# A state-space layer on one core: a logarithm in place of a polynomial step, a sixth product a chunk on GpSimd, and a new timetable

## The chip, the core and the metric

The kernel runs on one core of one Trainium2 chip. The metric is device time in microseconds of one execution. The kernel before takes 4875.83 us (median of 3 runs, 4874.54 to 4876.55). The engines are named as in the profile: PE (TensorE), DVE (VectorE), ACT (ScalarE), POOL (GpSimd) and SP (SyncE, which here only issues transfers).

## What is computed

Two layers follow each other on x of shape (2, 512, 64, 64). Each is `x = x + layer(groupnorm(x))`. Layer 0 is a selective scan over the 4096 positions of an image, with 1024 channels and 16 states for each channel:

```python
xs = silu(conv1d(layernorm(x) @ in_proj_x))       # z = layernorm(x) @ in_proj_z
dt, B, C = split(xs @ x_proj)
delta = softplus(dt @ dt_proj + dt_bias)
h = exp(delta * A) * h + (delta * xs) * B          # for each position, in order
y = sum_n(h * C) + xs * D
x = x + (y * silu(z)) @ out_proj
```

Layer 1 matches each position with 1024 memory rows (scores, softmax, arg-max), adds the positions into the rows chosen, and multiplies the softmax with the renewed rows. The change leaves layer 1's own code as it was.

## The kernel before

**Tiling of layer 0.** The positions are cut into 32 chunks of 256 (16 for each image; `chunks`, T = 256). Channels lie on the 128 partitions in 8 blocks (`DB`), states in 4 groups of 4 (`G`, `NG`). A *unit* is one channel block and one state group of one chunk: 4 states x 256 positions, a tile of 128x1024. So a chunk has 32 units, and its units are called 0 to 31 here. Blocks go in pairs `p` (8 units each).

**One unit k** takes, in the order of the main loop:

- ACT, `decay(k+1)`: four exponentials write dA of the next unit into PSUM (pool `psa`, two buffers). One unit ahead.
- at the first unit of a pair, `turn`: ACT copies the finished sums yT of the pair before to `ys`, PE transposes them into `py`.
- at unit 2 of a pair (`AT["gate"]`), `gate`: DVE multiplies `py` with silu(z).
- everything that `table` has due at this unit (below).
- DVE, `scan(k)`: `tensor_tensor_scan` runs h = dA*h + bu in place over dA. Then DVE multiplies with C (`weigh`) into `hc` (pool `t2`, two buffers). ACT copies the last column of h to `carry`.
- PE, `gather(k)`: eight transposes of `hc` accumulate in yT.
- POOL, `feed(k+4)`: bu = B * (delta*u) for the unit four ahead (pool `fed`, four buffers, so it must wait for `scan(k)`).
- ACT, `first(k+3)`: copies four first columns into bu.
- POOL, `start`, at units 3, 11, 19, 27: delta*u of the next pair, and its first columns.

**Units set aside.** In units 2, 8, 12, 16 and 26 (`AT["aside"]`) DVE only scans. The scan writes h to an SBUF tile (tag `dS`, one buffer), and POOL multiplies it with C one unit later into an `hc` buffer; PE gathers it right after that unit's own gather.

**Everything else of a chunk** (projections of the next chunk, the norm of the one after it, the output projection of the one before) is cut into parts with due times in units, in the dictionary `AT`; a negative time lies before the chunk's start. `table` is sorted by due time and then priority, and a wrapper (`InOrder`) keeps each engine's instructions in the order in which the loop issues them, SP's transfers too. Parts that matter here: `"u"`, `"z"` (projections on PE, 16 matmuls each), `"c"` (convolutions, 16 matmuls), `"xi"`, `"o"`, `"zo"` (their ACT copies), `"silu"` 9 (ACT loads another function table, takes the silu of z and u, and loads the first table again), `"norm"` (load of x, group norm on ACT in two halves, mean, centre, two squares, variance, root, Newton step, scale), `"back"` (output projection), `"soft"` (delta; its eight times are repeated every 8 units). B and C of the next chunk are loaded at units 26 to 32, as soon as the last reader of each buffer is done.

**delta.** softplus(x) = relu(x) + log(1 + e), e = exp(-|x|). The kernel takes the logarithm on ACT into PSUM (`lg`), and for small e, where 1 + e loses digits, a cubic series; DVE takes the lesser of both (`d_min`). The series is an ACT Square and two POOL instructions (`d_series`). `pd`, `lg` and `py` share one PSUM buffer (pool `psy`, tag `py`).

Of the kernel before, what the change touches and what calls it, by code (L numbers as in the profile page):

```python
# [2 lines left out]

# [6 lines left out]
F32 = mybir.dt.float32  # L10
# [3 lines left out]
AF = mybir.ActivationFunctionType  # L14
ALU = mybir.AluOpType
# [4 lines left out]
P = 128  # L20
# [30 lines left out]
def kernel(  # L51
# [17 lines left out]
    nc = tc.nc  # L69
    B, C, L = x.shape  # L70
    CB = C // P
# [6 lines left out]
    T = 256  # L78
    NCH = L // T
    NG = 4  # L80
# [7 lines left out]
    const = ctx.enter_context(tc.tile_pool(name="const", bufs=1))  # L88
# [16 lines left out]
        out=g3, in_=g3, compare_op=ALU.is_ge, fill=0.0, base=GS - 1,  # L105
        pattern=[[GS, P // GS], [0, GS]], channel_multiplier=-1,
    )
    one = const.tile([P, 1], F32, name="one")
    nc.gpsimd.memset(one, 1.0)
    epsc = const.tile([P, 1], F32, name="epsc")  # L110
    nc.gpsimd.memset(epsc, EPS)
    serb = const.tile([P, 1], F32, name="serb")
    nc.gpsimd.memset(serb, -0.75 * 3.0**-0.5)


    win = const.tile([P, CB, 2 * DI], F32, name="win")
# [8 lines left out]
    xf0 = flat[:, : CB * TT].rearrange("p (c t) -> p c t", t=TT)  # L125
# [4 lines left out]
    gmu = [[const.tile([P, CB], F32, name=f"gmu{i}_{b}") for b in range(B)] for i in range(2)]  # L130
    grs = [[const.tile([P, CB], F32, name=f"grs{i}_{b}") for b in range(B)] for i in range(2)]
# [55 lines left out]
    with ExitStack() as l0:  # L187
        nc = InOrder(tc, tc.nc)
# [1 line left out]


        AT = {
            "u": (-10, -7, -2, 0), "xi": (-9, -6, 1, 2), "c": (-6, -3, 3, 5), "o": (-4, -1, 4, 7),
            "x": 10, "xo": 12, "z": (16, 18, 19, 23), "zo": (18, 19, 22, 27),
            "soft": (20, 21, 22, 22, 22, 24, 25, 26), "silu": 9, "early": -114,
            "aside": (2, 8, 12, 16, 26), "gate": 2,
            "norm": (-1, 0, 3, 8, 10, 10, 11, 14, 15, 17, 18, 18),
            "back": ((0, 6, 8, 10), (1, 13, 14, 15)), "end": 23, "u1": (4, 5, 9, 10),
# [5 lines left out]
        }  # L204
        wp = l0.enter_context(tc.tile_pool(name="w0", bufs=1))
# [4 lines left out]
        t2 = l0.enter_context(tc.tile_pool(name="t2", bufs=2))  # L210
        fed = l0.enter_context(tc.tile_pool(name="fed", bufs=LEAD))
        dl = l0.enter_context(tc.tile_pool(name="dl", bufs=DB // 2 - 1))
        s1 = l0.enter_context(tc.tile_pool(name="s1", bufs=1))
# [36 lines left out]
        U = DB * G  # L250
# [207 lines left out]
        def front(i):  # L458
# [94 lines left out]

            def d_exp(p):
                e = s["e", p]
                nc.scalar.activation(e, e, AF.Exp, scale=-1.0)
                s["q", p] = s1.tile([P, 2, T], F32, tag="q", name="q")
                nc.scalar.activation(s["q", p], e, AF.Square, bias=serb, scale=3.0**-0.5)

            def d_series(p):  # L560
                q = s["q", p]
                engine = nc.vector if i == 0 and p == 0 else nc.gpsimd
                engine.tensor_scalar(q, q, 1.0, 0.8125, ALU.mult, ALU.add)
                engine.tensor_mul(q, q, s["e", p])

            def d_log(p):
                lg = psy.tile([P, 2, T], F32, tag="py", name="lg")
                s["lg", p] = lg
                nc.scalar.activation(lg, s.pop(("e", p)), AF.Ln, bias=one)

            def d_min(p):
                q = s["q", p]
                nc.vector.scalar_tensor_tensor(
                    q, s.pop(("lg", p)), 1.25 * 2.0**-23, q, ALU.add, ALU.min
                )

            def d_sum(p):
# [199 lines left out]
        def prelude():  # L777

            def load_n():
                nc.sync.dma_start(xf0, x1d[0][:, :, :TT])  # L780
                nc.sync.dma_start(mn, mnd)
                nc.sync.dma_start(mrow, m.rearrange("(kb p) c -> p kb c", p=P))

            def norm():
                for cb in range(CB):
                    nc.gpsimd.tensor_scalar(
                        xf0[:, cb], xf0[:, cb], gmu[1][0][:, cb : cb + 1],
                        grs[1][0][:, cb : cb + 1], ALU.subtract, ALU.mult,
                    )

            def turn(i):
                pt = ps.tile([P, 2, T], F32, tag="mm", name="pt")
                pt = pt.rearrange("p a t -> p (a t)")
                for cb in range(CB):
                    nc.tensor.transpose(
                        pt[:, cb * P : (cb + 1) * P], xf0[:, cb, i * P : (i + 1) * P], ident
                    )
                nc.scalar.copy(xT0[:, i], pt)
                junk = s1.tile([P, 2, T], F32, tag="sq", name="junk")
                nc.scalar.activation(  # L800
                    junk.rearrange("p a t -> p (a t)"), xT0[:, i], AF.Square,
                    accum_out=ss0[:, i : i + 1],
                )
# [49 lines left out]
        def early(k):  # L853

            return k % U == AT["early"]

        def aside(k):

            return early(k) or k % U in AT["aside"]

        def decay(k):
            i, db, g = units[k]
# [12 lines left out]
        def scan(k):  # L875
            i, db, g = units[k]
            b, c = chunks[i]
            dA, bu = dAs[k], bus.pop(k)
            if aside(k) and not early(k):
                dAs[k] = s1.tile([P, NG, T], F32, tag="dS", name="h")  # L880
            h = dAs[k]
            nc.vector.tensor_tensor_scan(
                h.rearrange("p n t -> p (n t)"), dA.rearrange("p n t -> p (n t)"),
                bu.rearrange("p n t -> p (n t)"), 0.0, ALU.mult, ALU.add,
            )
            if not aside(k):
                weigh(k, nc.vector)
            if c < NCH - 1:
                nc.scalar.copy(carry[:, db, g * NG : (g + 1) * NG], h[:, :, T - 1])


            if db % 2 == 0 and g == 0:
                pys[i, db // 2] = psy.tile([P, HT, 2, P], F32, tag="yT", name="yT")
            if g == 0:
                for hf in range(HT):
                    nc.tensor.matmul(
                        pys[i, db // 2][:, hf, db % 2], u_of(i, db)[:, hf * P : (hf + 1) * P],
                        dD[:, db], start=db % 2 == 0 and hf == 0, stop=False,
                        skip_group_check=True,
                    )  # L900

        def weigh(k, engine):

            i, db, g = units[k]
            hcs[k] = t2.tile([P, NG, T], F32, tag="hc", name="hc")
            engine.tensor_mul(hcs[k], dAs.pop(k), state[i]["C"][g])

        def gather(k):

            i, db, g = units[k]  # L910
            hc = hcs.pop(k)
            for n in range(NG):
# [120 lines left out]
        for k, (i, db, g) in enumerate(units):  # L1033
            w = k % U
            if k + 1 < n_units and not early(k + 1):
                decay(k + 1)
            if w % (2 * G) == 0 and k > 0:
                turn(*((i, w // (2 * G) - 1) if w else (i - 1, PR - 1)))
            late = i == 0 and w // (2 * G) == 1
            if w % (2 * G) == AT["gate1" if late else "gate"] and k >= 2 * G:  # L1040
                gate(*((i, w // (2 * G) - 1) if w >= 2 * G else (i - 1, PR - 1)))
            while table and table[0][0] <= k:
                table.pop(0)[2]()
            if k + 4 < n_units and early(k + 4):
                decay(k + 4)
            scan(k)
            if k > 0 and aside(k - 1):
                weigh(k - 1, nc.gpsimd)
            for n in (k, k - 1):
                if n in hcs:  # L1050
                    gather(n)
            if k + LEAD < n_units:
                feed(k + LEAD)
            if k + LEAD - 1 < n_units:
                first(k + LEAD - 1)
            if (k + 5) % (2 * G) == 0 and k + 5 < n_units:
                start(units[k + 5][0], units[k + 5][1] // 2)
# [493 lines left out]
```

## Time and profile before

| | |
|---|---|
| median of the runs | 4875.83 us |
| the profiled execution | 4875.14 us |
| its span, first to last instruction | 4872.8 us (2.3 us lie around it) |
| granted clock | 0.981 |
| busy over the span | PE 90%, DVE 87%, POOL 81%, ACT 75% |
| before the first scan | 100.0 us |
| chunk 0 / chunks 1 to 30 / chunk 31 | 143.8 / 3519.4 / 129.2 us |
| after the last scan (mostly layer 1) | 980.4 us |

Names in the profile read `out<-in`: `hc<-dA,C` is the product with C on DVE, `hc<-h,C` the one of a unit set aside on POOL, `dA<-dA,bu` a scan, `h<-dA,bu` the scan of a unit set aside, `bu<-B,du` a feed, `z<-py,z` a gate, `x<-x,pm` the centring of x. L37 is the line of the wrapper, through which nearly everything of layer 0 is issued, so groups are told apart by their tiles. "Idle before" is time in which an engine did nothing ahead of an instruction, put down to what ended it.

### The profile page before, as it was taken

What the parts mean: (1) busy time and instruction counts of PE and PEld (TensorE: products, weight loads), DVE (VectorE), ACT (ScalarE), POOL (GpSimd) and SP (SyncE); (2) the same over time, 40 slices, a digit from 0 to 9 for tenths busy, and PEclk for the clock granted to TensorE, in tenths of its full rate; (3) what the DMA queues carried; (4) which work ended last, traced back from release to release, by engine and by line L of the source; (5) the groups of instructions that cost most, each with busy time, mean ns of one, the idle gap of its engine ahead of it and who ended that gap; (6) DMA issues with size and microseconds to landing.
All of it is one profiled execution on the core that took longest, in us unless ns stands there. A gap on an engine that the chain in (4) does not pass through costs nothing. (4 is left out here: it accounts for less than half of the span.)

```text
span 4872.8 us, 65401 instructions
## 1 busy us (share of the span) xinstructions
PE 4407.3 (90%) x22660; PEld 3440.9 (71%) x22660; DVE 4223.4 (87%) x3538; ACT 3633.0 (75%) x9311; POOL 3971.2 (81%) x2753
## 2 busy tenths in 40 slices
PE   7899999999989999989999899999897799998999
PEld 6777777777777777777777777777776644553444
DVE  6799999999999999999999999999999788887333
ACT  3788888888888888888888888888888555552000
POOL 4799999999999999999999999999999745553121
PEclk9999999999999999999999999999998799999999
DMA  6132222222222222211221122222222134444442
GB/s 220 42 112 70 66 66 66 67 71 70 74 72 70 70 70 72 68 66 66 66 66 66 66 68 73 75 76 73 77 69 87 53 129 164 155 156 162 168 177 104
DMA packets 175348, 439.37 MB, mean 90 GB/s; under 512 B 23688, under 2 KB 78088, under 8 KB 171304
## 3 DMA queue, kind: packets, MB, share of 16 engines
q1 hardware_dynamic: 160456, 366.89, 22.6%
q0 software_dynamic: 10240, 34.61, 2.0%
q10 hardware_dynamic: 4320, 33.69, 1.9%
q8 instruction: 178, 2.92, 0.2%
q14 instruction: 154, 1.26, 0.1%
HBM read 347.44 MB, written 87.69 MB: 89 GB/s over the span
## 5 line engine op out<-in xcount | busy, mean ns | idle before, releaser
L37 POOL TENSOR_TENSOR bu<-B,du 128x1020 f32<-128x1020 f32 (+1 forms) x1151 | 2460.7, 2154 | 131.0 <-DVE dA L37 73.7
L37 ACT ACTIVATE dA<-delta,A 128x256 f32<-128x256 f32 x4096 | 1957.0, 478 | 137.9 <-DVE hc L37 32.9
L37 DVE TENSOR_TENSOR_SCAN dA<-dA,bu 128x1024 f32<-128x1024 f32 x864 | 1975.7, 2287 | 24.8 <-ACT dA L37 18.2
L37 PE MATMUL yT<-ident,hc 128*128 128x128 f32 x8192 | 1076.4, 278 | 185.1 <-DVE hc L37 110.8
L37 DVE TENSOR_TENSOR hc<-dA,C 128x1024 f32<-128x1024 f32 x864 | 1058.3, 1225 | 112.9 <-PE yT L37 18.6
L37 PEld LDWEIGHTS yT<-ident,hc 128*128 128x128 f32 x8192 | 941.8, 143 | 299.7 <-DVE hc L37 153.7
L37 PE MATMUL pz<-x,win 128*128 128x256 f32 x4096 | 942.3, 384 | 21.6 <-ACT carry L37 19.6
L37 PEld LDWEIGHTS pz<-x,win 128*128 128x128 f32 x4096 | 769.1, 193 | 125.3 <-ACT carry L37 25.9
L37 PE MATMUL cv<-xi,cd 128*128 128x256 f32 x2048 | 468.6, 381 | 32.1 <-ACT xi L37 30.3
L37 PE MATMUL po<-z,wo 128*128 128x256 f32 x2048 | 472.9, 384 | 0.8 <-DVE z L37 0.8
L37 PEld LDWEIGHTS cv<-xi,cd 128*128 128x128 f32 x2048 | 379.5, 190 | 88.2 <-ACT xi L37 37.2
L37 PEld LDWEIGHTS po<-z,wo 128*128 128x128 f32 x2048 | 386.6, 193 | 53.7 <-DVE z L37 1.0
L37 POOL TENSOR_TENSOR hc<-h,C 128x1024 f32<-128x1024 f32 x160 | 385.0, 2407 | 3.9 <-PE yT L37 3.9
L37 DVE TENSOR_TENSOR_SCAN h<-dA,bu 128x1024 f32<-128x1024 f32 x160 | 364.4, 2278 | 3.6 <-ACT dA L37 3.6
L37 ACT COPY carry<-dA 128x4 f32<-128x4 f32 x810 | 128.6, 159 | 226.4 <-DVE hc L37 220.1
L37 PE MATMUL py<-ident,ys 128*128 128x128 f32 x512 | 87.7, 296 | 158.6 <-ACT ys L37 156.6
L37 ACT COPY bu<-bu 128x4 f32<-128x4 f32 x1024 | 204.1, 200 | 35.7 <-POOL bu L37 35.7
L1483 POOL TENSOR_TENSOR xt<-xt,cd 128x1024 f32<-128x1024 f32 x7 | 16.4, 2348 | 232.0 <-DMA xt<-x1d 125.1
L1479 ACT COPY cd<-A 128x1024 f32<-128x1024 f32 x7 | 7.1, 1012 | 244.9 <-PE A L1428 244.9
L37 PEld LDWEIGHTS py<-ident,ys 128*128 128x128 f32 x512 | 55.7, 145 | 189.2 <-ACT ys L37 187.0
L1177 POOL DMA_INDIRECT tab<-rows,ix x64 | 70.3, 1098 | 144.3 <-DVE rows L1175 97.9
L37 PEld LDWEIGHTS yT<-dD,u 128*128 128x128 f32 x1024 | 146.1, 196 | 43.9 <-issue 38.7
(261 smaller groups left out, 6297.4 us busy)
## 6 DMA issues: line engine op xcount, KB each, us to landing
B<-bcd SPq DMA_DIRECT2D x128, 512.0 KB, 3.8
C<-bcd SPq DMA_DIRECT2D x128, 512.0 KB, 4.2
wo<-in_out_wT_dram SPq DMA_DIRECT2D x128, 512.0 KB, 4.9
exd<-exT ACTq DMA_DIRECT2D x14, 2048.0 KB, 7.0
exT<-exd SPq DMA_DIRECT2D x14, 2048.0 KB, 9.0
xl<-in_x_dram SPq DMA_DIRECT2D x32, 512.0 KB, 6.5
x<-in_x_dram SPq DMA_DIRECT2D x32, 512.0 KB, 5.1
xo<-in_x_dram SPq DMA_DIRECT2D x64, 256.0 KB, 4.9
```

What stands on the lines that cost most here:

```text
L37: ins = call(*args, **kwargs)
L1177: nc.gpsimd.indirect_dma_start(tab, at, rows, None)
L1479: nc.scalar.copy(one_s, A)
L1483: nc.gpsimd.tensor_add(x22, x22, vee)
```

## The change

Four things are edited, all in layer 0. (1) The series: POOL's `tensor_scalar` falls away, ACT's Square becomes a second Ln, and the three activations get other constants, held in [128,1] tiles; e now carries a factor 3/8. DVE's instruction changes its operations only. (2) A unit set aside is multiplied with C in place, over h, and gathered two units after its scan; there are six such units a chunk and eight in the last chunk. (3) x is loaded at unit -7 in place of -1. (4) Due times move. In the norm of the last chunk (`prelude`) the subtract-and-multiply becomes multiply-and-add, with two small instructions ahead of it.

```diff
@@ constants: one, serb go; part = log(3/8), padeb = beta0, under = 1 - 3*2**-24 come
+    beta0 = math.exp(-8.0 / 3.0)
...
         AT = {
-            "u": (-10, -7, -2, 0), "xi": (-9, -6, 1, 2), "c": (-6, -3, 3, 5), "o": (-4, -1, 4, 7),
-            "x": 10, "xo": 12, "z": (16, 18, 19, 23), "zo": (18, 19, 22, 27),
-            "soft": (20, 21, 22, 22, 22, 24, 25, 26), "silu": 9, "early": -114,
-            "aside": (2, 8, 12, 16, 26), "gate": 2,
-            "norm": (-1, 0, 3, 8, 10, 10, 11, 14, 15, 17, 18, 18),
-            "back": ((0, 6, 8, 10), (1, 13, 14, 15)), "end": 23, "u1": (4, 5, 9, 10),
+            "u": (-10, -7, -2, 0), "xi": (-8, -6, 1, 2), "c": (-6, -3, 1, 5), "o": (-4, -1, 4, 7),
+            "x": 10, "xo": 12, "z": (16, 18, 19, 26), "zo": (18, 19, 22, 27),
+            "soft": (20, 21, 22, 23, 23, 25, 26, 27), "silu": 9, "early": -114,
+            "aside": (1, 5, 9, 13, 24, 29), "aside_end": (1, 5, 9, 13, 17, 21, 25, 28), "gate": 3,
+            "norm": (-7, 3, 3, 9, 10, 10, 11, 15, 15, 17, 18, 18),
+            "back": ((0, 6, 9, 10), (1, 13, 14, 15)), "end": 23, "u1": (4, 5, 9, 10),
...
-            "wo": (6, -4, 9, 7), "m": (7, 12, 17, 23, 28, 29), "gs": 11, "zo1": (2, 4, 5, 7),
+            "wo": (6, -2, 9, 7), "m": (7, 12, 17, 23, 28, 29), "gs": 11, "zo1": (2, 4, 5, 7),
@@ d_exp
-                nc.scalar.activation(e, e, AF.Exp, scale=-1.0)
+                nc.scalar.activation(e, e, AF.Exp, bias=part, scale=-1.0)
...
-                nc.scalar.activation(s["q", p], e, AF.Square, bias=serb, scale=3.0**-0.5)
+                nc.scalar.activation(
+                    s["q", p], e, AF.Ln, bias=padeb, scale=beta0 * 32.0 / 9.0
+                )
@@ d_series
-                engine.tensor_scalar(q, q, 1.0, 0.8125, ALU.mult, ALU.add)
                 engine.tensor_mul(q, q, s["e", p])
@@ d_log
-                nc.scalar.activation(lg, s.pop(("e", p)), AF.Ln, bias=one)
+                nc.scalar.activation(
+                    lg, s.pop(("e", p)), AF.Ln, bias=under, scale=8.0 / 3.0
+                )
@@ d_min
-                    q, s.pop(("lg", p)), 1.25 * 2.0**-23, q, ALU.add, ALU.min
+                    q, q, -1.0, s.pop(("lg", p)), ALU.mult, ALU.max
@@ prelude, norm
+                sh = s1.tile([P, CB], F32, tag="gs_d", name="sh1")
+                nc.gpsimd.tensor_mul(sh, gmu[1][0], grs[1][0])
+                nc.gpsimd.tensor_scalar(sh, sh, -1.0, 0.0, ALU.mult, ALU.add)
...
-                        xf0[:, cb], xf0[:, cb], gmu[1][0][:, cb : cb + 1],
-                        grs[1][0][:, cb : cb + 1], ALU.subtract, ALU.mult,
+                        xf0[:, cb], xf0[:, cb], grs[1][0][:, cb : cb + 1], sh[:, cb : cb + 1],
+                        ALU.mult, ALU.add,
@@ aside
-            return early(k) or k % U in AT["aside"]
+            return early(k) or k % U in AT["aside" if k // U < last else "aside_end"]
@@ weigh
-            hcs[k] = t2.tile([P, NG, T], F32, tag="hc", name="hc")
-            engine.tensor_mul(hcs[k], dAs.pop(k), state[i]["C"][g])
+            h = dAs.pop(k)
+            hcs[k] = h
+            if not aside(k):
+                hcs[k] = t2.tile([P, NG, T], F32, tag="hc", name="hc")
+            engine.tensor_mul(hcs[k], h, state[i]["C"][g])
@@ main loop, after scan(k)
+            for n in (k, k - 2):
+                if n in hcs:
+                    gather(n)
             if k > 0 and aside(k - 1):
                 weigh(k - 1, nc.gpsimd)
-            for n in (k, k - 1):
-                if n in hcs:
-                    gather(n)
```

More of the change, by code (lines that the diff above doesn't have):

```diff
@@ L1 @@
 import itertools
+import math
 from contextlib import ExitStack
@@ L107 @@
     )
-    one = const.tile([P, 1], F32, name="one")
-    nc.gpsimd.memset(one, 1.0)
     epsc = const.tile([P, 1], F32, name="epsc")
     nc.gpsimd.memset(epsc, EPS)
-    serb = const.tile([P, 1], F32, name="serb")
-    nc.gpsimd.memset(serb, -0.75 * 3.0**-0.5)
+    beta0 = math.exp(-8.0 / 3.0)
+    part = const.tile([P, 1], F32, name="part")
+    nc.gpsimd.memset(part, math.log(3.0 / 8.0))
+    padeb = const.tile([P, 1], F32, name="padeb")
+    nc.gpsimd.memset(padeb, beta0)
+    under = const.tile([P, 1], F32, name="under")
+    nc.gpsimd.memset(under, 1.0 - 3.0 * 2.0**-24)
     win = const.tile([P, CB, 2 * DI], F32, name="win")
```

## The prediction, as put on record before the result

> **What bounds the kernel now.** I read first the busy times by stage. Layer 0's chunks 1 to 30 fill 3519.4 of 4872.8 us, 117.1 to 117.7 us each (chunk 16, which also holds the second image's statistics, 120.2), and all look like this one:
>
> ```profile
> core 0: us, PE busy (x) PEld busy (x) DVE busy (x) ACT busy (x) POOL busy (x), PEclk, DMA share, GB/s
> 2123.00:2240.10 117.10, 105.57 (x619) 90.89 (x617) 111.11 (x74) 103.42 (x271) 111.70 (x74) 1.00 0.21 69
> ```
>
> DVE is idle for 6.0 us, POOL 5.4, PE 11.5, ACT 13.7. No engine has room to spare, so each edit must be asked whom it loads. Then the groups by line, DVE and POOL:
>
> ```profile
> L37 DVE TENSOR_TENSOR_SCAN dA<-dA,bu 128x1024 f32<-128x1024 f32 x864 | 1975.7, 2287 | 24.8 <-ACT dA L37 18.2 <-POOL bu L37 1.3
> L37 DVE TENSOR_TENSOR hc<-dA,C 128x1024 f32<-128x1024 f32 x864 | 1058.3, 1225 | 112.9 <-PE yT L37 18.6 <-DVE dA L37 2.7 <-POOL bu L37 0.5
> L37 DVE TENSOR_TENSOR_SCAN h<-dA,bu 128x1024 f32<-128x1024 f32 x160 | 364.4, 2278 | 3.6 <-ACT dA L37 3.6
> L37 POOL TENSOR_TENSOR hc<-h,C 128x1024 f32<-128x1024 f32 x160 | 385.0, 2407 | 3.9 <-PE yT L37 3.9
> ```
>
> 112.9 us of idle before 864 products is about 0.1 us each, the step from a scan to its product; it returns 27 times a chunk (2.7 of DVE's 6.0 us) and is no wait for another engine. In the waits, only two of DVE's stalls in these chunks are large:
>
> ```profile
> DVE z L37 <- ACT z L37: 62.2, 31, 3.8
> ...
> DVE q L37 <- POOL q L37: 23.5, 27, 1.1
> ```
>
> That is 2.0 us a chunk at the gate of unit 10 (z waits for its silu) and 0.9 at unit 24. So DVE sets the pace of these chunks, with ACT in one stretch. That stretch in order of time, chunk 17, DVE from the product of unit 9 and ACT from the exponentials of unit 10:
>
> ```profile
> 2155.64 1.23 DVE L37 TENSOR_TENSOR hc<-dA,C 128x1024 f32<-128x1024 f32 x1
> 2158.82 0.69 DVE L37 TENSOR_TENSOR z<-py,z 128x512 f32<-128x512 f32 x1 [1.96 <-ACT z L37]
> 2159.43 1.21 DVE L37 TENSOR_TENSOR x<-x,pm 128x1024 f32<-128x1024 f32 x1
> 2160.56 2.29 DVE L37 TENSOR_TENSOR_SCAN dA<-dA,bu 128x1024 f32<-128x1024 f32 x1
> 2162.95 1.23 DVE L37 TENSOR_TENSOR hc<-dA,C 128x1024 f32<-128x1024 f32 x1
> 2164.31 2.30 DVE L37 TENSOR_TENSOR_SCAN dA<-dA,bu 128x1024 f32<-128x1024 f32 x1
> ```
>
> ```profile
> 2153.58 2.00 ACT L37 ACTIVATE dA<-delta,A 128x256 f32<-128x256 f32 x4
> 2155.59 1.28 ACT L37 ACT_TABLE_LOAD   x1
> 2156.88 1.91 ACT L37 ACTIVATE z<-z 128x2048 f32<-128x2048 f32 x1
> 2158.70 1.99 ACT L37 ACTIVATE u<-u 128x1024 f32<-128x1024 f32 x2
> 2160.71 1.28 ACT L37 ACT_TABLE_LOAD   x1
> ...
> 2162.20 2.01 ACT L37 ACTIVATE dA<-delta,A 128x256 f32<-128x256 f32 x4
> ```
>
> The silus hold ACT for 6.4 us (2155.59 to 2162.00). Unit 11's exponentials come behind them and end at 2164.21; DVE's scan of unit 11 starts at 2164.31, 0.1 later. So the gate's 1.96 us stall costs nothing of its own: without it, DVE would wait as long for unit 11's exponentials.
>
> **The change, part by part.** A chunk is counted from the end of its predecessor's last product. In chunk 17 that is 2122.47, so unit 11 starts scanning at 41.84, and the rest of the chunk takes 75.24.
>
> *Sixth product to POOL.* DVE starts scans 3.53 us apart in a unit with a product (2143.41 to 2146.94) and 2.19 in one set aside (2151.07 to 2153.26): 1.34 us less DVE work. POOL gains 2.41 us.
>
> *Series.* POOL loses 4 x 0.618 us and four gaps of about 0.08, 2.8 in all, so its chunk goes from 111.7 to 111.3 us. The stall at unit 24 (0.92) goes: POOL's part is due at 23 and DVE's at 25, two units apart as now, but it is 0.7 us shorter and its ACT input is made a unit earlier (POOL waits 16.3 us for that in all now). ACT: Ln of this width has a row only into PSUM, 673 ns; Square into SBUF takes 723, so -50 to +50 ns for the exchange; I take nothing, since Ln and Exp of 256 columns share one row at 417 ns. Exp gains a bias tile: e without one takes 615 ns, q with one 723, so 0 to +108 ns; I take 0.1, 0.4 us a chunk. The Trainium skill (ScalarE: Activation LUTs, What ACT_TABLE_LOAD costs) puts each such operand at about 93 ns.
>
> *Gate to unit 3 of a pair.* Nothing by itself, by the two fences above: the stall reappears as scan <- dA.
>
> *Where the sixth unit lies.* Units 1, 5, 9 replace 2 and 8, so the saved 1.34 us lies ahead of unit 11, where ACT decides. The walk: DVE work to unit 5's scan end is 4 x 3.53 (units 0, 2, 3, 4) + 2.19 (unit 1, its scan's end included in the pitch) + 0.60 (`q`) + 0.60 (gate) + 2.3, so 19.8. ACT cannot copy unit 5's carry before that. It is itself later: both halves of the group norm (2 x 1.0) and the two small exponentials (0.4) now fall in unit 3, where ACT has 1.3 us to spare (3.53 less 2.0 for the exponentials and 0.2 for two copies), and I get 20.7 against 21.06 now (2143.53). From unit 5's carry to the end of unit 11's exponentials ACT ran 20.68 us with under 0.1 us of waiting, and the change leaves the same instructions there plus 0.1. So unit 11 scans at about 41.5, 0.3 earlier, while DVE alone would be there at 38.4: a stall of about 3 us that shows as DVE dA <- ACT dA. The table loads in this stretch take 1.28 us and the next activation starts 0.01 us later. The same section of the Trainium skill makes a switch 2.66 us, with a drain; by it the silus would last 2.8 us longer in both kernels, and the difference would be the same.
>
> *Behind unit 11* both versions have three units aside, so only the 0.9 us goes: 75.24 - 0.9 = 74.3.
>
> *In place, one buffer.* New waits: POOL's product overwrites h, so it waits for ACT's carry (unit 9's stands behind the silus at about 39, the product's turn is 38.3; up to 1 us, and POOL waits for unit 11's scan at 43.7 anyway; `feed` stands behind it with four units of lead). The scan of the next unit aside writes the same tile, so DVE waits for PE's gather, two units after the scan, where it only needed POOL's product before. From 24 to 29: PE does u (3.45 us) at 25, z and a convolution (6.9) at 26, then gathers 26 and 24. I get 105.7 for that against 106.0 for the scan. From 29 to the next chunk's 1: 118.8 against 119.4. From 1 to 5, 5 to 9, 9 to 13 PE is 1.5 to 2 us early. Tight twice; I charge 0.2 us a chunk, between nothing and, at 2 us of lateness, 3.1 us.
>
> *PE's turn.* `lg` is now freed at unit 1 of a pair, after the transposes of `py` are issued at unit 0; they use the same buffer. PE waits for DVE's `q`, at 0 and 16 about 1.5 us more than now (2.29 after the chunk's first scan now, `q` ends 4.1); at 8 PE is later anyway (by 2.9), at 24 DVE's unit has no product, so `q` comes early. PE has 11.5 us idle, so its chunk of 105.6 + 5 for the copies of yT + 3 still fits in 115.8. I take nothing.
>
> *x at -7.* Its buffer's last reader is the z projection, now at unit 26, so the SP queue stands at this load until about 100.6; behind it wait B's four loads, whose first is now issued at 95.4 (2218.34 less 2122.98). B lands 3.8 us after issue, x 5.1, so B's first lands at 104.8 to 107.7; POOL's feed wants it at 106.3 (the feed's turn, after `start`). POOL waits 0 to 1.4 us and has over 4 us of lead there; I take nothing, 1.4 at worst. xo and wo gain room that they do not need.
>
> **The sum.** A chunk: 41.5 + 74.3 + 0.2 = 116.0 against 117.1, 1.1 us less. 30 chunks: 33 us. Last chunk: three more products, 3 x 1.34 = 4.0, shortened by POOL's norm there (four instructions of 2.1 us in a row, behind which PE waited 13.4 us for a product and DVE 8.5); I take 3, from -5 to +12. First chunk: 0.5. Layer 1: nothing. 36.5 off the profiled 4875.1 gives **4839 us**, 0.7% less; the median of the runs is 0.7 us from the profiled execution. With both small costs at their worst (3.1 + 1.4 a chunk, against 1.3 gained) it would be 4875 + 30 x 3.2 - 3.5, 4968.
>
> **Rivals.**
> *DVE decides everywhere.* If ACT gets ahead of unit 5, the 3 us stall goes. A chunk is then 117.1 - 1.34 - 2.0 - 0.9 = 112.9, POOL's 111.3 just fits; 30 x 4.2 + 5: 4745. For it: ACT idles 13.7 us a chunk. Against: those lie behind unit 11; between 5 and 11 it has none. A half-way case gives 4790. Chance 0.13.
> *POOL behind late B.* The feed waits 1.4 us, and with 111.3 + 1.4 and the waits for DVE at units 11 and 17 its lead is not regained: the gain per chunk falls to 0.2, 4866 to 4884. For: POOL's idle of 5.4 is mostly waiting for scans. Against: four buffers of lead. Chance 0.17.
> *The h tile makes DVE wait for PE (slower).* Place: scans of 29 and 1 behind gathers 24 and 29. Price: each microsecond of PE's lateness beyond 0.3 and 0.6 us goes to DVE. It decides from about 1 us of lateness, where both waits together (1.1) eat the gain; at 2 us the chunk loses 3.1 - 1.3 = 1.8, 4875 + 54 = 4929. For: PE's idle of 11.5 us is nearly all waiting for `ys` and products, and two projections now lie at 25 and 26. Against: unit 23 has lost one. Chance 0.20.
> *The forecast*, 4805 to 4866: 0.50.
>
> The range reaches down to the half-way case and up past the POOL case into the near part of the slower one, 4790 to 4890; about 0.1 of the chance lies on either side. A measurement of this kernel tells 0.2% (10 us) from no change. Faster by more: 0.50 + 0.13 + 0.05 of the POOL case; within: 0.12; slower: 0.20.
>
> **What would show it.** Right: chunks of about 116 us; DVE's wait z <- ACT z gone and dA <- ACT dA of 2.5 to 3.5 us a chunk in its place; q <- POOL q gone; POOL busy near 111; SP's B loads in one burst after x, near unit 26. Wrong: h <- PE yT waits of over 1 us a chunk, bu <- DMA B at POOL, or a chunk near 113 with no wait at unit 11.

## The result: half a per cent slower

| | before | after |
|---|---|---|
| median of 6 runs each, us | 4875.70 (4871.75 to 4877.23) | 4900.39 (4890.16 to 4908.57) |
| profiled execution, and its span | 4875.14, 4872.8 | 4896.73, 4894.8 |
| start to first scan, chunk 0 | 100.0, 143.8 | 98.4, 143.8 |
| chunks 1 to 30 together | 3519.4 | 3541.8 |
| chunk 31, and all behind it | 129.2, 980.4 | 128.1, 982.7 |

The ratio is 1.005 (95% interval 1.0034 to 1.0065). The forecast was 4839, the range 4790 to 4890: the time lies outside it and on the other side of no change. The span grew by 22.0 us, and chunks 1 to 30 by 22.4; the other parts nearly cancel. Busy times of these chunks in the changed kernel:

```profile
core 0: us, PE busy (x) PEld busy (x) DVE busy (x) ACT busy (x) POOL busy (x), PEclk, DMA share, GB/s
242.30:3784.10 3541.80, 3199.06 (x18431) 2791.97 (x18429) 3303.66 (x2137) 3104.74 (x8093) 3341.64 (x2139) 0.97 0.20 70
```

Before, the same stretch had DVE busy for 3333.45 us, POOL for 3353.23, and a granted clock of 0.99. So the work did come off DVE, 29.8 us of it, but DVE's idle time rose by 52.2. Whom it waits for stands in DVE's waits of the changed kernel (whole span: us in total, times, longest):

```profile
DVE x L38 <- PE pm L38: 109.3, 32, 6.4
...
DVE q L38 <- POOL q L38: 29.9, 35, 2.6
DVE hc L38 <- PE yT L38: 27.2, 14, 2.8
DVE dA L38 <- ACT dA L38: 21.0, 10, 4.1
```

The wait for ACT's silu (62.2 us before) is gone, as forecast. In its place is not ACT's dA, but PE's `pm`, the mean for a later chunk's norm, which stands on PE behind `py`. The wait for `q`, which the change was to remove, is longer than before (23.5). GpSimd now waits for B's transfers 46 times, where it had a single such wait of 4.1 us:

```profile
POOL bu L38 <- DMA B<-bcd: 50.3, 27, 4.6
...
POOL bu L38 <- DMA B<-b0d: 28.7, 19, 3.7
```

The stretch that leads to `x <- pm` in order of time, chunk 17, whose first scan starts at 2138.1; POOL first, then PE, then DVE:

```profile
2163.35 2.38 POOL L38 TENSOR_TENSOR h<-h,C 128x1024 f32<-128x1024 f32 x1
2165.68 2.42 POOL L38 TENSOR_TENSOR bu<-B,du 128x1020 f32<-128x1020 f32 x1
2167.99 1.33 POOL L38 TENSOR_TENSOR q<-q,e 128x512 f32<-128x512 f32 x1
```

```profile
2166.01 1.04 PE L38 MATMUL yT<-ident,h 128*128 128x128 f32 x8
2170.19 0.93 PE L38 MATMUL py<-ident,ys 128*128 128x128 f32 x4 [3.14 <-DVE q L38]
2170.91 1.06 PE L38 MATMUL yT<-dD,u 128*128 128x128 f32 x4
2171.77 1.91 PE L38 MATMUL yT<-ident,hc 128*128 128x128 f32 x8
2173.47 2.05 PE L38 MATMUL pm<-x,meanc 128*128 128x256 f32 x8
```

```profile
2169.35 0.69 DVE L38 SCALAR_TENSOR_TENSOR q<-q,lg 128x512 f32<-128x512 f32 x1 [0.80 <-POOL q L38]
2169.96 2.28 DVE L38 TENSOR_TENSOR_SCAN h<-dA,bu 128x1024 f32<-128x1024 f32 x1
2175.56 1.22 DVE L38 TENSOR_TENSOR x<-x,pm 128x1024 f32<-128x1024 f32 x1 [3.32 <-PE pm L38]
```

In the kernel before, the same turn of chunk 17 was on PE:

```profile
2153.36 0.65 PE L37 MATMUL py<-ident,ys 128*128 128x128 f32 x4 [1.66 <-ACT ys L37]
2153.86 1.89 PE L37 MATMUL pm<-x,meanc 128*128 128x256 f32 x8
```

It is a chain of waits. `q` now comes at unit 1 of a pair and reads `lg`, whose buffer `py` needs. So PE's turn waits for DVE's `q`. On DVE `q` has its place behind the product of unit 8, which ends at 2168.56, and then waits another 0.80 us for POOL's part, which stands behind the product of unit 5. PE idles for 3.14 us, where it idled for 1.66 before, until ACT's copy `ys` came, and then runs at half its clock, as the busy times before, in and behind the stretch show (granted clock third from the end):

```profile
2163.80:2170.40 6.60, 3.35 (x28) 2.83 (x27) 5.70 (x5) 6.18 (x18) 6.60 (x4) 1.00 0.27 79
2170.45:2173.86 3.41, 3.41 (x18) 3.37 (x17) 1.79 (x1) 3.38 (x3) 3.41 (x2) 0.51 0.00 0
2174.00:2180.00 6.00, 6.00 (x30) 5.17 (x29) 4.41 (x3) 5.87 (x12) 6.00 (x4) 1.00 0.02 3
```

`py` takes 0.93 us there instead of 0.65, and DVE waits 3.32 us for `pm`. Between `py` and `pm` now stand two groups of unit 8 that were behind `pm` before; the reason comes with e4 below. By the trace's clock records, chunks 1 to 30 hold 193.7 us of half clock, against 65.9 before. A second place is units 23 to 26, again on PE:

```profile
2228.08 1.09 PE L38 MATMUL yT<-ident,hc 128*128 128x128 f32 x8 [1.65 <-DVE hc L38]
2230.94 0.63 PE L38 MATMUL py<-ident,ys 128*128 128x128 f32 x4 [1.77 <-DVE q L38]
...
2236.18 3.62 PE L38 MATMUL pz<-x,win 128*128 128x256 f32 x16
2239.64 3.62 PE L38 MATMUL cv<-xi,cd 128*128 128x256 f32 x16
```

With the last z product gone from unit 23, PE has gaps at 23 and 24, and then a product and a convolution in a row at 26, 7.1 us, ahead of the transposes of units 26 and on.

### The profile page after: what moved, and what is told of

Read it like the earlier page. It is cut to its first block, busy times and chain, and to the rows that moved or that the text cites. A ratio compares the mean times of both kernels' runs of the same rounds, so it can differ in the third digit from the quotient of the medians.

```text
span 4894.8 us, 65626 instructions
## 1 busy us (share of the span) xinstructions
PE 4422.8 (90%) x22660; PEld 3490.8 (71%) x22660; DVE 4191.8 (86%) x3503; ACT 3634.4 (74%) x9311; POOL 3956.5 (81%) x2663
## 5 line engine op out<-in xcount | busy, mean ns | idle before, releaser
L38 DVE TENSOR_TENSOR_SCAN dA<-dA,bu 128x1024 f32<-128x1024 f32 x830 | 1899.8, 2289 | 33.2 <-ACT dA L38 21.0
L38 DVE TENSOR_TENSOR hc<-dA,C 128x1024 f32<-128x1024 f32 x830 | 1016.8, 1225 | 100.9 <-PE yT L38 27.2
L38 PE MATMUL yT<-ident,hc 128*128 128x128 f32 x6640 | 892.4, 281 | 153.9 <-DVE hc L38 150.7
L38 PEld LDWEIGHTS yT<-ident,hc 128*128 128x128 f32 x6640 | 780.6, 145 | 234.1 <-DVE hc L38 196.8
L38 POOL TENSOR_TENSOR h<-h,C 128x1024 f32<-128x1024 f32 x194 | 460.7, 2375 | 8.9 <-DVE h L38 4.5
L38 DVE TENSOR_TENSOR_SCAN h<-dA,bu 128x1024 f32<-128x1024 f32 x194 | 442.6, 2281 | 16.7 <-PE yT L38 16.7
L38 PE MATMUL yT<-ident,h 128*128 128x128 f32 x1552 | 206.5, 277 | 5.1 <-POOL h L38 5.1
```

The lines of the kernel that those rows point to most:

```text
L38: ins = call(*args, **kwargs)
```

## The experiments

The theories. **A**: `q` at unit 1 makes PE's turn wait. **B**: x's load at -7 stands on SP ahead of B's and keeps POOL waiting. **C**: a product saved ahead of unit 11 is worth nothing, for ACT's silus set the pace there. **D**: the last z product at 26 leaves PE idle at 22 to 25 and overfull behind. Rival to A and D: the lower clock itself is the cost, not the order of PE's work. All ratios are to the kernel before on the same chip (medians there 4868 to 4876 us). The chips differ by up to 8 us, so kernels of different rows are better compared by the ratio. The chunk is the median of chunks 1 to 30; DVE's waits are totals over these.

| kernel | us | ratio, 95% interval | chunk | DVE's waits, us |
|---|---|---|---|---|
| the change | 4900 | 1.0034 to 1.0065 | 117.4 | pm 99, q 27, yT 23, dA 6 |
| e1, delta's steps back | 4907 | 1.0051 to 1.0075 | 118.8 | dA 77, yT 52, pm 36 |
| e2, x at -1 | 4883 | 1.0006 to 1.0024 | 117.3 | pm 73, yT 51, dA 23 |
| e5, filler on PE | 4954 | 1.0153 to 1.0180 | 119.6 | pm 104, dA 66 |
| e6, delta's steps and z back | 4871 | 0.9985 to 1.0003 | 116.8 | dA 83, pm 35 |
| e7, z back | 4883 | 1.0008 to 1.0026 | 117.3 | dA 77, pm 63 |
| e13, e6 and x at -1 | 4870 | 0.9983 to 1.0001 | 116.8 | dA 83, pm 34 |
| e4, before with delta's new steps | 4956 | 1.0155 to 1.0181 | 119.8 | dA 74, z 65, yT 35 |
| e9, before with the series | 4849 | 0.9937 to 0.9964 | 116.2 | z 60, dA 5 |
| e10, series, in place | 4841 | 0.9919 to 0.9947 | 116.1 | z 63, dA 14 |
| e8, e10 and a sixth product at 20 | 4900 | 1.0043 to 1.0071 | 117.9 | z 71, q 67, dA 33 |
| e11, sixth at 0 | 4950 | 1.0140 to 1.0168 | 119.3 | yT 101, z 98 |
| e12, sixth at 0, own tile | 4879 | 1.0002 to 1.0020 | 117.1 | POOL hc 62, z 59 |
| e14, products at 0, 4, 8, 12, 16, 26 | 4839 | 0.9914 to 0.9941 | 116.1 | z 59, yT 37, dA 18 |
| e16, sixth at 30, own tile | 4903 | 1.0042 to 1.0070 | 117.9 | z 59, dA 61, yT 22 |
| e15, e10 with the change's six places | 4957 | 1.0148 to 1.0176 | 120.0 | z 99, dA 78, yT 32 |
| e19, e15 and the convolution at 1 | 4936 | 1.0115 to 1.0149 | 119.3 | z 100, dA 74 |
| e17, e10 and gate 3 | 4840 | 0.9924 to 0.9951 | 116.1 | dA 72 |
| e18, e14 and gate 3 | 4832 | 0.9914 to 0.9941 | 115.7 | dA 78, yT 29 |

### Taking pieces of the timetable back

e1, e2 and e5, each from the changed kernel:

```diff
-            "soft": (20, 21, 22, 23, 23, 25, 26, 27),      # e1
+            "soft": (20, 21, 22, 22, 22, 24, 25, 26),
-            "norm": (-7, 3, 3, 9, ...                      # e2
+            "norm": (-1, 3, 3, 9, ...
+            if p in (0, 2):                                # e5, ahead of py
+                fill = ps.tile([P, 2, T], F32, tag="mm", name="fill")
+                for n in range(12 if p == 0 else 6):
+                    nc.tensor.matmul(fill[:, 0], ident, win[:, 0, :T], start=True, stop=True)
```

> The kernel after, with only delta's due times put back to those of before (DVE's q at unit 0 of a pair, not 1). Theory A (the turn): after, PE's transposes into py wait for DVE's q, because lg holds their PSUM buffer a unit longer (113.8 us of PE idle in chunks 1 to 30); PE's clock falls, the mean comes late and DVE's centring waits 98.5 us for it. Then here that wait is under 25 us, half-clock time in chunks 1 to 30 is under 90 us (after 194, before 66), DVE waits at unit 11 for ACT instead, and the time is 4825 to 4845. Theory B (the load of x): POOL is late because B stands behind x on the SP queue (44 us of waits for B and 26 us for its first column), and q is late because of POOL. Then the wait for the mean stays over 60 us and the time is 4880 to 4900.

> The kernel after, with only the load of x put back to unit -1. Theory A: POOL's 70 us of waits for B vanish, but they lay beside DVE's waits; the wait for the mean stays over 80 us; the time is within 15 us of the kernel after, 4885 to 4905. Theory B: the wait for the mean and q <- POOL q fall with them, time 4840 to 4865.

> The kernel after, with 12 matmuls (2.6 us) without use ahead of PE's transposes into py at unit 8 and 6 (1.3 us) at unit 24, into a PSUM buffer that is free there. They fill the idle stretch and take no wait away. If the fall of PE's clock after the idle stretch is what makes the mean late, half-clock time in chunks 1 to 30 falls from 194 to under 110 us, the wait for the mean from 3.3 to about 1.8 us a chunk, and the time is 30 to 50 us below after. If the wait for q alone does it, the time is within 10 us of after, whatever the clock does.

e1 shows A's mechanism right and its price wrong. The wait for `pm` falls from 99 to 36 us and ACT's dA comes up behind it, 77 us, most of it at unit 11 (2.35 us a chunk, where the prediction had put about 3). But the time, expected at 4825 to 4845 us, doesn't fall, for the second place takes over, with 52 us of waiting for yT where it was 23 (the lines give the whole span, the table chunks 1 to 30):

```profile
DVE dA L38 <- ACT dA L38: 94.2, 50, 4.5
...
DVE hc L38 <- PE yT L38: 58.1, 28, 2.9
...
DVE x L38 <- PE pm L38: 47.0, 32, 6.4
```

e2 shows that B holds, at a smaller price: POOL's waits for B are down to a single one of 4.6 us outside these chunks, and the kernel is 17 us faster. That lies between the ranges of the two theories, for the wait for `pm` falls only to 73 us and the one for yT rises to 51. e5 was to test the rival, the clock. It keeps the clock up (50 us of half clock, from 194) and the mean in chunks 1 to 30 at full:

```profile
242.00:3784.00 3542.00, 3318.88 (x19282) 2906.44 (x19281) 3248.32 (x2101) 3061.91 (x7975) 3296.96 (x2109) 1.00 0.20 69
```

It is 54 us slower than the change all the same. But the added matmuls of unit 8 take 5.35 us a chunk in its trace, not the expected 2.6, more than the idle 3.14 us that they were to fill, so e5 makes PE late itself (the wait for `pm` stays at 104) and does not test the clock alone. So a clock kept up by added work was worth less than the work cost. What the low clock adds can be read beside it: from the start of `py` to the end of `pm` PE takes 5.3 us in the change and 3.7 in e5, e6 and e13 (medians of these chunks), where the clock is full there. By this estimate about 1.7 of the 3.3 us that DVE waits for `pm` are the clock's part, so the rival is true in part.

e6, e7 and e13, again from the changed kernel (the load and copy behind `"xi"` had to go back with z):

```diff
-            ..., "xi": (-8, -6, 1, 2), ...     # e6, e7, e13
+            ..., "xi": (-9, -6, 1, 2), ...
-            ..., "z": (16, 18, 19, 26), ...
+            ..., "z": (16, 18, 19, 23), ...
-            "soft": (20, 21, 22, 23, 23, 25, 26, 27),   # e6, e13
+            "soft": (20, 21, 22, 22, 22, 24, 25, 26),
-            "norm": (-7, 3, 3, 9, ...                   # e13
+            "norm": (-1, 3, 3, 9, ...
```

> The changed kernel with two pieces of its timetable put back: delta's steps one unit earlier from the fourth on (as before), and the last z product with its convolution at unit 23 instead of 26 (the second x transpose's load is put back with it). What is left of the change is the logarithm, the in-place product and the placement of six products. Theory D (the z product moved to 26 leaves TensorE idle over units 22 to 25, its clock falls, and at 26 it has double work, so the product of unit 28 waits for its tile) together with theory A (delta's later steps make VectorE wait for the transpose of unit 10): both stretches are mended, the waits for pm and for yT fall below 1 us a chunk, half-clock time over chunks 1 to 30 below 90 us from 194, what is left is the wait for ScalarE's dA of unit 11 at about 2.5 us: a chunk of 116.2 to 116.8, 4840 to 4865 us. Rival (x's load at unit -7 holds B back, theory B): B's waits at GpSimd stay at 1 to 2 us a chunk whatever TensorE does, and the time stays at 4890 to 4910.

> The changed kernel with only the last z product and its convolution back at unit 23 (and the second x transpose's load with it); delta's later steps stay. Theory D alone: the waits for yT at unit 28 (0.8 us a chunk) and the low clock at units 23 to 25 go; since the last z product ends earlier, x's load ahead of B on the queue is issued earlier too, and B's waits at GpSimd (70 us over chunks 1 to 30) should fall below 20. The wait for pm at unit 10 stays at about 3 us a chunk. Sum: 4865 to 4885 us. If delta's later steps alone cost the time (theory A), it stays at 4890 to 4905.

> The changed kernel with delta's steps, the last z product and x's load all put back to where the kernel before had them; of the timetable only the six products (units 1, 5, 9, 13, 24, 29), the gate at 3 and the third xo turn stay. Theory A and D with B: B's waits are gone already with z at 23, so x's load changes nothing more: within 0.2% of 4871. If x's load at unit -7 still costs (GpSimd does x's scaling earlier, in its fuller stretch), 4850 to 4862.

D holds: z at 23 alone gives 18 us back (e7), and on top of e1 it gives 35 (e6), with the wait for yT down from 52 to 1 us and the half clock from 173 to 54. B's waits go with it though x's load stays at -7, and putting x back as well changes nothing (e13). So the late B needed both: x's place ahead of B on the queue (e2), and the z product at 26, which holds x's buffer (e6, e7). e6 stands 6 us above the range that I had expected, level with the kernel before, and the waits left in it are those that the prediction had forecast for the whole change, and `pm` (whole span):

```profile
DVE dA L38 <- ACT dA L38: 99.6, 75, 4.5
...
DVE x L38 <- PE pm L38: 45.9, 32, 6.4
```

e4 puts delta's new steps into the kernel before and nothing else:

```diff
-            "soft": (20, 21, 22, 22, 22, 24, 25, 26),
+            "soft": (20, 21, 22, 23, 23, 25, 26, 27),
```

> The kernel before, with only delta's due times of the kernel after (q at unit 1 of a pair). Theory A: PE's transposes into py wait for DVE's q here too, about 1.5 to 3 us in two or three turns a chunk, half-clock time rises to over 130 us, the centring waits for the mean, and the time is 20 to 70 us above before. Theory B: nothing holds B back here, the time is within 10 us of before.

There the piece that "takes nothing" costs 83 us by itself (before, on this chip: 4873.5), more than theory A's 20 to 70. Besides `ys` (170.0 us, 156.6 before), PE's `py` now waits 108.1 us for DVE's `q` and 44.5 for ACT's dA, and the half clock rises from 66 to 263 us.

But one part of theory A fails in e4: DVE does not wait for `pm` at all. What grows in chunks 1 to 30 is its wait for ACT's dA, from 5 to 74 us, and for yT, from 3 to 35. PE and then DVE in chunk 17 of e4:

```profile
2195.26 1.11 PE L37 MATMUL py<-ident,ys 128*128 128x128 f32 x4 [3.27 <-ACT ys L37]
2196.16 2.88 PE L37 MATMUL pm<-x,meanc 128*128 128x256 f32 x8
```

```profile
2200.54 0.69 DVE L37 TENSOR_TENSOR z<-py,z 128x512 f32<-128x512 f32 x1 [2.19 <-ACT z L37]
2201.15 1.21 DVE L37 TENSOR_TENSOR x<-x,pm 128x1024 f32<-128x1024 f32 x1
```

`py` is as late as in the change, and `pm` still ends 2.1 us ahead of its use. Part of that is the gate: its wait for z stands ahead of the centring here and no longer does in the change. Without it the centring could have started at 2198.35 and would have waited some 0.7 us for `pm`, by an estimate from these rows, and not the change's 3.3. The rest is a due time that none of the theories names: in `"norm"` (its fourth number) the change also moves the mean from unit 8 to 9, behind unit 8's gather on PE, and leaves the centring at 10. In every kernel here with the mean at 9 (the change, e1, e2, e5, e6, e7, e13) DVE waits 34 to 104 us for `pm` in chunks 1 to 30; in every kernel with it at 8 it waits at most 1.3 us, in e17 and e18 too, which have the gate at 3 like the change. So the wait for `pm` goes with the mean at 9, and the late turn makes it longer. No run moves the mean alone, so what that step costs in time is open.

### Building up from the kernel before

e9 has only the logarithm's lines of the diff; e10 adds the in-place product and the gathers ahead of it; both keep the old timetable and five products.

> The kernel before with its own timetable and only the logarithm series (five products on GpSimd, their own tiles, the order before the gather as it was). If the series is worth the stall it removes at unit 24 (0.75 us a chunk over chunks 1 to 30, and 2.8 us of GpSimd's time each chunk, which moves nothing): chunk 116.2, 4845 to 4855 us. If what stands beside it takes the place of the stall (ScalarE's silus, the transposes), within 0.2% of 4875.

> The kernel before with its own timetable, the logarithm series, and the in-place product with gathers ahead of it (five products on GpSimd at the old units). It parts the two things by which the kernel with the product at unit 20 differs from the one with the series alone (4900 against 4849 us). If in place costs (h's tile comes free only after the gather two units later, gathers come later): 4870 to 4900. If it is the sixth product at unit 20, which stands ahead of delta's q on GpSimd (2.4 us wait there at unit 23): within 0.2% of the series alone, 4840 to 4858.

The series brings 25 us. POOL is busy for 109.3 us a chunk, from 111.7, and DVE's stall for it is gone; the chunk is 1.0 us shorter, where the prediction had 0.9. With these five places, in place costs nothing: the two intervals overlap, and e10's is the lower. The next runs add a sixth product to these:

```diff
-            "aside": (2, 8, 12, 16, 26), ...
+            "aside": (2, 8, 12, 16, 20, 26), ...   # e8
+            "aside": (0, 2, 8, 12, 16, 26), ...    # e11; e12 with own tiles
+            "aside": (0, 4, 8, 12, 16, 26), ...    # e14
+            "aside": (2, 8, 12, 16, 26, 30), ...   # e16, own tiles
+            "aside": (1, 5, 9, 13, 24, 29), ...    # e15; e19 also "c": (-6, -3, 1, 5)
-            ..., "gate": 2,                        # e17 (from e10), e18 (from e14)
+            ..., "gate": 3,
```

> The kernel before with its own timetable, with the logarithm, the in-place product after the gather and a sixth product on GpSimd, put at unit 20, where VectorE sets the pace. Theory C (of the change's parts the product saves its 1.34 us and the series its stall of 0.7 us only behind unit 11; ahead of it ScalarE sets the pace): chunk 117.1 less 1.34 less 0.9, 114.9 us, 30 such chunks: 4795 to 4825 us. Rival 1 (GpSimd becomes late: the sixth product delays the series of delta or the next bu): waits on q or bu of 1 us and more a chunk, 4850 to 4880. Rival 2 (in place, h's tile comes free late and VectorE's next dA or TensorE's clock suffers): 4880 to 4900.

> The series, in place, and the sixth product at unit 0 in place of unit 20: there GpSimd has slack (with the series alone it waits 1.6 us for VectorE at unit 3, 0.3 at 0, 0.3 at 9 and 2.4 at 10 and 11), while the stretch from unit 12 to 24 has none. If the place decides: the wait for q at unit 23 goes, VectorE saves 1.2 us at unit 1, ahead of the gate at unit 2 behind which ScalarE's silus start: chunk 116.15 less 1.2, about 115.0, 4808 to 4825 us. Rival (the silus that VectorE awaits at unit 9 don't move with it): the wait there grows from 2.0 to 3.2 and the time is that of five products, 4840 to 4858. Rival (in place or GpSimd late): 4865 and more.

> As the run with the sixth product at unit 0, but each product into its own tile and the order ahead of the gathers as before. If in place costs nothing, both within 0.2% of each other; if it costs 0.2 us a chunk as the prediction charged, this one is 6 us faster; if it costs over 1 us a chunk, 30 us and more.

> The kernel before with series and in-place product (4841 us with five products), and six products at units 0, 4, 8, 12, 16 and 26: never closer than four units, so that the tile that a product on GpSimd holds (one buffer) is free again. With products at 0 and 2 VectorE waited 3.3 us at unit 2 for it. If that spacing is the price: the wait at unit 2 goes, and VectorE has 1.2 us less at unit 1. Either ScalarE's silu at unit 9 moves with it (4805 to 4825 us) or VectorE waits there for it (2.0 us a chunk becomes 3.2, and the time is 4835 to 4850). I hold the second for likelier.

> The kernel before with the series, own tiles, and a sixth product at unit 30, behind which GpSimd's slack at units 0 and 3 (1.9 us a chunk) follows: VectorE does 1.2 us less at unit 31, and nothing is behind it but the transposes. If the product pays where VectorE sets the pace and GpSimd has slack: 4849 less 30 times 1.2, 4810 to 4822 us. If ScalarE's silu at unit 9 doesn't move with it, or TensorE's transposes of unit 30 come later than the turn at unit 0 wants them: 4845 to 4870.

No place pays clearly. At 20, where DVE sets the pace, POOL has no room: chunk 20 of e8, POOL and then DVE.

```profile
2575.32 2.37 POOL L38 TENSOR_TENSOR h<-h,C 128x1024 f32<-128x1024 f32 x1
2577.63 2.40 POOL L38 TENSOR_TENSOR bu<-B,du 128x1020 f32<-128x1020 f32 x1
2579.97 1.30 POOL L38 TENSOR_TENSOR q<-q,e 128x512 f32<-128x512 f32 x1
```

```profile
2581.30 0.69 DVE L38 SCALAR_TENSOR_TENSOR q<-q,lg 128x512 f32<-128x512 f32 x1 [2.40 <-POOL q L38]
```

The product stands ahead of `q`, and the wait it makes is 2.40 us, as long as the product itself, for 1.2 us saved. At 0, two units ahead of the next product, DVE waits for the one h tile: 3.3 us a chunk in place (until PE has gathered), 2.1 with own tiles (until POOL is done). There in place does cost: e11 is 71 us slower than e12. Spaced by four (e14) most of this goes, and the chunk is e10's to the tenth, so the second branch of its expectation held, though not by the wait for z, which stayed at 2.0 us a chunk: the time saved came back as waiting for yT, 1.1 us in 29 of 32 waits, nearly all at unit 8. At 30 PE's gather, with the turn behind it, waits 2.6 us for POOL's product at the chunk's start, and its clock falls there (211 us of half clock).

> The kernel before with series and in-place product, and of the change's timetable only the six places (1, 5, 9, 13, 24, 29); gate, loads, delta's steps and z products as before. If the places of the six products cost what parts 4871 (the change with its steps put back) from 4841 (series, in place, five products): 4865 to 4885, with a wait of VectorE for ScalarE at units 9 to 11 of 3 us a chunk and more, and one for q behind the products at 13 or 29. If they are worth the product (1.2 us a chunk): 4800 to 4820.

> The six new places in the old timetable (4957 us) with one more piece of the change: the convolution of the second pair at unit 1 instead of 3. With the places alone TensorE is idle for 4.3 us at unit 3 before it, its clock falls (half rate over 3.4 to 6.8 us of nearly every chunk), and VectorE waits 2.6 us for ScalarE's dA at unit 2 and 3.3 us at unit 9. If the idle stretch of TensorE is what made the places cost 116 us against five products: the idle time and the low clock at units 2 and 3 go, and 4885 to 4915 remain, with the wait at unit 9 unchanged. If it is ScalarE (the norm's part at unit 0, the gate at 2): TensorE's idle time goes and the time stays at 4940 to 4960.

The change's six places, alone, cost 116 us against e10, and the late convolution only some 15 to 20 of these. e19 lies between its two expected ranges: with the convolution at 1, PE's idle stretch of 4 us at unit 3 is gone, but one of 2.0 us stands at unit 4, and the half clock stays at 163 us. Among what else the change had moved with the places is the norm's part from unit 0 to 3, and the trace shows a reason for it. In e15 chunk 20 starts at 2526.7; SP's queue, then ACT:

```profile
2522.67 3.85 SPq L38 DMA_DIRECT2D C<-bcd  x2
2526.62 0.39 SPq L38 DMA_DIRECT2D x<-in_x_dram  x1
2527.12 0.43 SPq L38 DMA_DIRECT2D C<-bcd  x1
```

```profile
2532.41 1.09 ACT L38 ACTIVATE x<-x,gsh,grs 128x256 f32<-128x256 f32 x2 [2.91 <-DMA x<-in_x_dram]
```

x's load stands on SP behind the third of C's four loads, which are let go as the products of the last units end. With a product of these on POOL, x goes out 0.1 us ahead of the chunk's first scan; in e10 it was 3.6 ahead. ACT waits for it (74 us in all, 1 in e10), and dA of unit 2 is late behind it. This wait is not there in e13, whose norm comes at 3, with x's load as late. No run moves the norm's part alone, so its share of the remaining 95 to 100 us is argued, not shown.

> The kernel with the series and the in-place product (4841 us, VectorE waits 2.1 us a chunk for ScalarE's silu at unit 9), with the gate from unit 2 to unit 3 of every eight. The prediction took this step at nothing: the silus move behind the dA of the next units, VectorE's wait for z goes and comes back as a wait for ScalarE's dA two units on. So: z > z from 2.1 to under 0.5 us a chunk, ACT dA > dA from 0.5 to about 2.5, and the time within 0.2% of 4841. If the gate is worth something by itself (it takes the silus out from ahead of VectorE's z product): 4800 to 4825 us.

> As the run with six products at 0, 4, 8, 12, 16, 26 (4839 us), with the gate at unit 3. If ScalarE sets the pace from the gate to unit 11 whatever stands ahead, the time stays within 0.2% of 4839 and the wait only changes its name. If the saving of the sixth product was held up by the silus at unit 9 and the gate frees it: 4800 to 4820 us.

e17 is what the prediction said of the gate: the wait for z goes (63 us to nothing), the wait for dA comes (14 to 72), and the time is the same. e18 is the best kernel here, 0.7% faster than before, but its interval is e14's and overlaps e10's: the sixth product and the gate together are not told apart from having neither. Side by side on one chip, where before took 4868 us, e18's five runs are 4827 to 4838 us and e17's 4836 to 4848, so a gain of some 8 us from the product is not ruled out.

## Why the prediction was wrong

Split at the start of unit 11's scan, as the sum is, chunks 1 to 30 take 41.9 + 75.4 us on average before and 42.9 + 75.2 in the change, where the forecast was 41.5 + 74.3 and 0.2 for in place. So most of the miss lies ahead of unit 11, where ACT was to set the pace and PE's `pm` did.

- **PE's turn ("I take nothing")** is the step that failed first. That `lg` is freed at unit 1 and PE waits for `q` was right, but not where: the prediction put the added wait at units 0 and 16 and none at 8 and 24. Measured, `py` waits 3.2 us a chunk at 8 (1.6 before) and 1.7 at 24 (1.0), and about as long as before at 0 and 16 (1.3 and 0.8). And it weighed PE's wait against PE's idle total of 11.5 us a chunk, while `pm`, which stands behind the turn, is awaited by DVE at once: 98 us in chunks 1 to 30, where the sum had nothing. Once z is back, delta's steps are worth 11 us (e7 against e6); put back alone they gain nothing (e1); in the kernel before they cost 83 (e4), there through ACT's dA and yT. The pieces don't add.
- **The mean from 8 to 9** is not in the prediction at all. Every long wait for `pm` here goes with it; its price was not measured.
- **The last z product from 23 to 26** was never priced as an edit; it came in only as work ahead of two gathers, under *In place*, at 0.2 us a chunk. It is worth 18 to 35 us (e7, e6): the largest piece.
- **x at -7 ("I take nothing, 1.4 at worst")**: 17 us by e2, 0.6 a chunk. That was within the bounds, and the rival *POOL behind late B* named it; the value chosen was wrong. POOL's waits for B come to 70 us, 2.3 a chunk, more than the 1.4 that the walk allowed; it counted B's issue, 95.4, from the chunk's first scan and not, like the rest, from the product before, 0.5 us earlier. With z back the waits are gone (e7).
- **Sixth product and its places.** The walk put unit 11 at 41.5 us, 0.3 earlier than before. With delta's steps, z and x put back (e13) it comes at 42.2, 0.3 later, and what follows takes 74.9. So the forecast of 116.0 a chunk owed nearly all to the series, and that e10, a kernel without the sixth product, measures 116.1 and 4841 bears out the series and not the walk. What was missed is that the product, its places and the rest of the timetable cost about 30 us even so (e13 against e10): 22 in chunks 1 to 30, in waits for dA and `pm`, 4 in the last chunk, the rest at the start. How the 22 us divide among the places, the gate, the norm's parts, the convolution and POOL I have not settled.
- **The last chunk**, taken at 3 us less, gained 1.1 (129.2 to 128.1); with the series alone it gains 6.9 (e9).
- **Series**: right, 1.0 us a chunk in e9. In the changed kernel too the stall at unit 24 is gone, and half of the chunks take 74.3 us behind unit 11; but `q` was given a later turn and now waits 0.9 us a chunk at unit 9.
- **Gate**: right (e17). **In place**: right that it is small, at five products (e10). The rival that made DVE wait for yT's gather shows in e11 (101 us) and, at 29 to 37 us, in e14, e15 and e18, but not in chunks 1 to 30 of the change.

The rival on the slower side had the right engine, PE, but the wrong wait: `h <- PE yT` is 16.7 us in all, none of it in chunks 1 to 30, and what decided was `x <- PE pm`.

On the clock: the Trainium skill (TensorE: Matmul & The Clock Gate, Part 1: The HAM clock gate) gives half rate after an idle window of about 3.4 us, and its section Why this matters for your kernels asks for no idle gap over some 3 us. The stretch shown above agrees with the second: a gap of 3.14 us, then 3.41 us at half clock. The low clock at unit 4 in e10 follows a gap of 1.4 us, with PE busy for 58 to 68% of the 3.4 us before it, so staying under 3 us of idle in one piece did not keep the clock here.

## What to carry to other kernels

When an edit makes an engine wait, don't compare the wait with that engine's idle total: look at the instruction queued right behind it and who awaits that within the next microseconds. Price every moved due time as an edit of its own, by the hole it leaves and the heap it makes, and by the buffer whose reuse holds a load, and all loads behind it on the queue. Look also for due times that moved without being named, as the mean's did. Where two engines are both near 111 of 117 us busy, look for a place where the giver sets the pace and the taker has room before moving work from one to the other; of the places tried here none gained clearly.

## What the hardware showed that I had not expected

PE's clock fell to half for 3.4 us, or a multiple of that, after idle gaps that need not be long: 1.4 us ahead of unit 4 in e10, 3.1 us in the change. In e10 that happens at unit 4 in 24 of 30 chunks (133 us of half clock in chunks 1 to 30, twice that of before), and it is among the fastest kernels; e13, with 47 us, is 30 us slower. So the total of half clock does not tell the time: what counted in these traces was whether PE's next result was awaited.

In every kernel here the stretches of half clock start on one grid with steps of 3.413 us, by the clock records. e10's chunk of 116.06 us is 34.0 such steps, so a gap that returns in every chunk falls on the same place of the grid, which fits its regular dips. In e9, where the same gap of 1.4 us stands ahead of unit 4, only one chunk in 30 has a dip there. So the length of a gap alone does not tell whether the clock falls.
